# Preparation spread over every second unit, and one running sequence of stages beside a selective-scan loop

## The chip, the cores and the metric

The kernel runs on one core of a Trainium2 chip. The core has a matrix engine (PE), a vector engine (DVE), a scalar engine (ACT), a general engine (POOL) and a queue engine (SP), which here issues almost all DMAs. Each engine works through its own list of instructions in order and waits on semaphores. The metric is device time in microseconds, from start to end of one execution; lower is better. Four timed executions of the kernel before lie between 13899.16 and 13924.62 us, median 13905.3 us.

## The reference

The input is x, float32 of shape (4, 96, 64, 64). Four layers are applied, each as x + layer(group_norm(x)) with 32 groups and no gains:

- layer 0: attention with 3 heads from all 4096 pixels to a 2x2-averaged grid, a 3x3 neighbourhood mix of its result, a 5x5 depthwise term and a projection;
- layer 1: a projection to 2 x 192 channels, a 3x3 depthwise convolution and SiLU, then a selective scan in four directions, a layer norm, a gate, a 1x1 / 3x3 depthwise / 1x1 chain and a squeeze-and-excite factor;
- layer 2: a 3x3 convolution of 96 to 96 channels;
- layer 3: pointwise and depthwise convolutions, a second four-direction scan, a gate, layer norms, a grouped squeeze/expand unit with a softmax over channels, and a projection.

The scans are the bulk. For each image, direction, channel (192) and state (16) a recurrence runs over 4096 positions:

```
h[t] = h[t-1] * exp(delta[t] * A) + delta[t] * u[t] * B[t]
y[t] = sum over 16 states of h[t] * C[t]   (plus a D term)
```

with delta = softplus(dt_w @ x_dbl + dt_b), and x_dbl, B, C from a projection of u. Layer 1 writes the same recurrence as a quotient of cumulative sums.

## The kernel before

There are eight scans, one per image and scan layer, in the order of `SCANS`: layer 1 of images 0 and 1, layer 3 of images 0 and 1, then the same of images 2 and 3. Each has 4 directions x 4 chunks of 1024 positions x 2 halves of the channels = 32 **groups** of 96 channels. A group has 12 **units**; one unit is 8 channels x 16 states = 128 partitions by 1024 positions. So a scan has 384 units and the loop 3072.

`unit(i, ...)` writes out by hand one turn of the loop for all engines:

- SP: `fetch(i + AHEAD)` loads one row block of delta, broadcast to 16 states, into a `rep` tile (L2038, 12 buffers, 512 KB); AHEAD is 4.
- ACT: `decays(i + 2)` makes exp(delta * A) in place (L2046); `carry_on` copies the last column (L2074).
- DVE: `scan(i)` (L2066), then `times_b(i + 1)` (L2059) multiplies the driven term, in PSUM, by B.
- POOL: `times_c(i)` (L2078) multiplies the states by C.
- PE: `drive(i + 2)` spreads delta * u to the partitions (two bf16 matmuls into `bx`); every fourth unit `collect` sums four finished units into `acc`. Once a group `output` moves `acc` to `yo`, and a store (L2114) takes `yo` to DRAM.

Two other streams are generators whose pieces are put between these by `Slots`: a `yield` ends a piece. **Preparation** (`prepare(g)`) makes the next groups' inputs: u is loaded (L1932, `load_u`), projected, and B, C go through DRAM (`rows`, `bc`); then delta is made by ACT (L1982 to L1988) and five POOL operations (L1989, L1991, L1995, L2006, L2009); delta goes to DRAM as `dd`, and delta * u, cut into three bf16 parts (`cut`, `cut2`), goes through `du` to `parts`. Tiles `t_`, `w_`, `delta` have one buffer each. It begins LEAD = 6 units before the end of group g - 2; DMAs are put off by `later(n, f)`, which runs f n units on. **Stages** (`first`, `second`, `third`, `last`) are the convolutional parts of the layers for other images, listed by scan in `BESIDE`. They take the PE time that `PACE[s]` leaves in a unit, in up to three slots per unit: at its head, after `times_b` (ahead of `collect` and `drive`) and after `drive`. A new `Slots` is made at the start of each scan; what is left of its stage is run out 19 units before the scan's end.

A stage's matmuls go to PSUM tiles tagged `one`, of which there are two; `held()` takes one of them for long in attention, `neighbours` and the layer norms. `group_norm_on_scalar` (L1161 on), `layer_norm` (L1261 on) and the gate of `second` (L1687, L1688) have DVE instructions that follow an ACT instruction in the same piece. `directions` (before `second` and `third`) loads the four direction sums of an image by `ungapped`, four DMAs of 24 partitions each (L1121), 64 DMAs in two pieces.

Of the kernel before, what the change touches and what calls it, by code (L numbers as in the profile page):

```python
# [20 lines left out]
R, N = 6, 16  # L21
# [19 lines left out]
PHI_EPS = 1e-12  # L41
PACE = (2.95,3.45,3.45,2.95,2.95,3.45,3.45,3.2)

# [857 lines left out]
def streams(ctx: ExitStack, tc: tile.TileContext, x, wts, cst, out, wat, cat, flag):  # L901
# [139 lines left out]
    def held():  # L1041

        return ps.tile([128, PCH], F32, tag="one", name="held")

# [73 lines left out]
    def ungapped(dst, src, cols):  # L1118

        for q in range(4):  # L1120
            nc.sync.dma_start(out=dst[24 * q : 24 * q + 24], in_=src[32 * q : 32 * q + 24, cols])  # L1121

# [36 lines left out]
    def group_norm_on_scalar(src, dst):  # L1161

        st = small.tile([96, 8], F32, name="gs_st")
        for j in range(4):
            s = src[:, bass.ts(j, CH)]
            nc.scalar.activation(s, s, AF.Copy, accum_out=st[:, j : j + 1])
            yield 1
        mv = small.tile([96, 4], F32, name="gs_mv")
        nc.vector.tensor_reduce(mv[:, 0:1], st[:, 0:4], AX.X, ALU.add)
        yield 0.5  # L1170
        p = bank()
        mm(p[:96, 0:1], group[:96], mv[:, 0:1])
        yield
        nc.scalar.activation(mv[:, 1:2], p[:96, 0:1], AF.Copy, scale=-1.0 / L)
        yield 0.5
        for j in range(8):
            p = bank()
            nc.scalar.activation(p[:96], src[:, bass.ts(j, PCH)], AF.Square, bias=mv[:, 1:2], accum_out=st[:, j : j + 1])
            yield 1
        nc.vector.tensor_reduce(mv[:, 2:3], st, AX.X, ALU.add)  # L1180
        yield 0.5
        p = bank()
        mm(p[:96, 0:1], group[:96], mv[:, 2:3])
        yield
        nc.scalar.activation(mv[:, 2:3], p[:96, 0:1], AF.Sqrt, bias=eps[:96], scale=1.0 / L)
        yield 0.5
        nc.vector.reciprocal(mv[:, 2:3], mv[:, 2:3])
        nc.vector.tensor_mul(mv[:, 3:4], mv[:, 1:2], mv[:, 2:3])
        yield 0.5
        for j in range(4):  # L1190
            nc.scalar.activation(dst[:, 16 * j : 16 * j + 16, :], img(src)[:, 16 * j : 16 * j + 16, :], AF.Identity,
                                 scale=mv[:, 2:3], bias=mv[:, 3:4])
            yield 1
# [67 lines left out]
    def layer_norm(pool, V, n, gains, each, chunks=range(8)):  # L1261
# [30 lines left out]
        nc.scalar.activation(r[:m], acc[:m], AF.Sqrt, bias=eps[:m])  # L1292
        yield n
        nc.vector.reciprocal(r[:m], r[:m])
# [12 lines left out]
    def attention(b, xn, samp, dist):  # L1307

        with Stack(2) as pool:
# [46 lines left out]
            for pair in [((0, e), (1, e)) for e in range(4)] + [((2, 0), (2, 1)), ((2, 2), (2, 3))]:  # L1356
# [24 lines left out]
                for s, (r, e) in enumerate(pair):  # L1381
# [3 lines left out]
                        rs[bass.ts(s, 32)].rearrange("p (a b) -> p a b", b=32),  # L1385
                    )
                yield 1
            yield from pool.clean()

    def neighbours(b, xn, samp, dist, feat):  # L1390


        with Stack(2) as pool:
# [36 lines left out]
            rs = lines[:8]  # L1430
            nc.vector.reciprocal(rs, acc[:8])
            yield 1
            for j in range(8):
# [74 lines left out]
    def directions(pool, b, tag):  # L1508

        V = pool.tile([96, 2, L], F32, name="V", bufs=1)  # L1510
        with Stack(1) as T:
            full = len(groups) // len(SCANS) * (SCANS.index((tag, b)) + 1)
            cols = []
            for h in range(2):
                while stored[0] < full - 1 + h:
                    yield WAIT
                t = T.tile([96, W, H], F32, name="yc", bufs=2)
                cols.append(t)
                for j in range(4):
                    ungapped(t.rearrange("p a b -> p (a b)")[:, bass.ts(j, CH)], y_col[h][b], bass.ts(j, CH))  # L1520
                    ungapped(V[:, h, bass.ts(j, CH)], y_row[h][b], bass.ts(j, CH))
                yield 4

# [18 lines left out]
    def second(b):  # L1542
# [90 lines left out]
        with Stack(1) as R2:  # L1633
# [32 lines left out]
            with Stack(2) as pool:  # L1666
# [3 lines left out]
                for j in range(8):  # L1670
# [15 lines left out]

                    nc.scalar.activation(q[:96], q[:96], AF.Tanh, bias=half_ag2, scale=0.5)  # L1687
                    nc.vector.scalar_tensor_tensor(out=x2, in0=q[:96], scalar=1.0, in1=x2, op0=ALU.add, op1=ALU.mult)  # L1688
                    nc.sync.dma_start(out=skip3[b][:, js], in_=x2)
# [31 lines left out]
    def last(b):  # L1721

        with Stack(1) as PX:
            V = PX.tile([96, 2, L], F32, name="V", bufs=1)
            per_way = 2 * NCH
            first_ = len(groups) - 4 * per_way
            while stored[0] < first_ + 2 * per_way:
                yield WAIT
            with Stack(1) as T:
                for h in range(2):  # L1730
                    t = T.tile([96, W, H], F32, name="yc")
                    for j in range(4):
                        ungapped(t.rearrange("p a b -> p (a b)")[:, bass.ts(j, CH)], y_col[h][b], bass.ts(j, CH))
                    yield 1
                    for j in range(8):
                        nc.scalar.copy(img(V[:, h, bass.ts(j, PCH)]),
                                       t[:, :, 8 * j : 8 * j + 8].rearrange("p a b -> p b a"))
                        yield 1
            yield from finish(PX, b, V, [(first_ + 3 * per_way + 2 * k + 2, (7 - 2 * k, 6 - 2 * k)) for k in range(NCH)])

    def finish(PX, b, V, blocks):

        with Stack(2) as pool:
# [55 lines left out]
            for need, chunks in blocks:  # L1799
                while stored[0] < need:  # L1800
                    yield WAIT
# [134 lines left out]
    def prepare(g):  # L1936

        s, b, tag, k, axis, back, c, h = groups[g]
        if h == 0:
            us = low.pop(g) if g in low else load_u(g)  # L1940
            yield 0

            p = bank()
# [6 lines left out]
            bc = sp.tile([128, 2, CH], F32, name="bc", bufs=2)  # L1950
            at = [slice(64 * e, 64 * e + R + 2 * N) for e in range(2)]
            for e in at:
                nc.scalar.copy(pr[e], p[e])  # L1953

            def to_rows():
                for e in range(2):
                    nc.sync.dma_start(out=rows[:, bass.ts(e, PCH)], in_=pr[at[e]])

# [5 lines left out]

            later(1, to_rows)
            later(3, to_bc)
            yield 2
            low[g + 1] = us, bc
        else:
            us, bc = low.pop(g)  # L1970
            yield 0
            yield 0
# [11 lines left out]
        nc.scalar.activation(w, t, AF.Identity, bias=one[:96])  # L1984
        yield 0
        nc.scalar.activation(delta, w, AF.Identity, bias=minus[:96])
# [3 lines left out]
        yield 0  # L1990
        nc.gpsimd.tensor_tensor(delta, w, t, ALU.add)  # L1991
        yield 0
        dd = dram.tile([96, CH], F32, name="dd", bufs=3)
        later(1, lambda: nc.sync.dma_start(out=dd, in_=delta))
        nc.gpsimd.tensor_tensor(t, delta, time(us[h], back, 0, CH), ALU.mult)  # L1995
        yield 0

        if h == 1 and g + 1 < len(groups) and groups[g + 1][0] == s:
            later(1, lambda: low.update({g + 1: load_u(g + 1)}))


        parts = cuts[g % 2]
# [3 lines left out]
        nc.gpsimd.tensor_tensor(t, t, c0, ALU.subtract)  # L2006
        yield 0
        nc.scalar.copy(c1, t)
        nc.gpsimd.tensor_tensor(c2, t, c1, ALU.subtract)  # L2009
        yield 0  # L2010
        du = dram.tile([96, 3, CH], BF16, name="du", bufs=2)
# [10 lines left out]

        later(1, to_du)
        later(3, to_parts)
        ready[g] = parts, dd, bc
# [89 lines left out]

    AHEAD, BEHIND, LEAD = 4, 2, 6
    DRIVE, SUM, SLOT = 0.43, 1.71, 0.5
    total = len(groups) * NG
    per = total // len(SCANS)
    store, waiting, stored, owed = [], [], [0], 0.0  # L2120

# [11 lines left out]
    def unit(i, prep, work, budget):  # L2133


        if i + AHEAD < total:
            fetch(i + AHEAD)
        while store:
            store.pop()()
            stored[0] += 1  # L2140
        catch_up(1)
        j = i - BEHIND - 3
        due = j >= 0 and j % 4 == 0
        left = budget - DRIVE - (SUM if due else 0.0)
        mine = 1 <= prep.slots <= 3
        left -= prep.begin(1.0) if mine else work.begin(left)
# [10 lines left out]
        work.end()  # L2157
        left -= work.begin(left)
        if due:
# [5 lines left out]
        if due and j % NG == NG - 4:  # L2165
            store.append(output(j))
        work.end()
# [5 lines left out]
    class Slots:  # L2173


        def __init__(self, stage):
            self.stage, self.open, self.slots = stage, False, 0

        def begin(self, left):

            if left < 0.3:
                return 0.0
# [3 lines left out]
            if v == WAIT:  # L2186
                return left
            while isinstance(v, tuple):
# [6 lines left out]
        def end(self):  # L2195
            if self.open:
                self.open = False
                next(self.stage, 0)

# [5 lines left out]

    def beside(s):
        stages = {"first": first, "second": second, "third": third, "last": last}
        for n, b in BESIDE[s]:
            yield from stages[n](b)

    Slots(first(0)).run()
    solo[0] = False
    with tc.manual_schedule():
# [15 lines left out]
        for i in range(total):  # L2229
            s, at = divmod(i, per)  # L2230
            g, m = divmod(i, NG)
            if at == 0:
                work, owed = Slots(beside(s)), 0.0
            if m == NG - LEAD and g + 2 < len(groups):
                prep.run()
                prep = Slots(prepare(g + 2))

            if at == per - NG - LEAD - 1 and s < len(SCANS) - 1:
                work.run()

            owed = min(owed, 0.6) + PACE[s]
            owed = unit(i, prep, work, owed)
        for j in range(total - 4, total, 4):
            collect(j)
            output(j)()
            stored[0] += 1
    solo[0] = True
    spare.clear()
    work.run()

# [48 lines left out]
```

## Time and profile before

| | |
|---|---|
| median of 4 runs | 13905.3 us |
| profiled execution, its own time | 13926.5 us |
| its span | 13924.7 us |
| before the first scan instruction | 661.6 us |
| loop of 3072 units | 661.6 to 13802.6 us |
| after the loop | 122.1 us |
| mean granted TensorE clock | 0.898 |
| DVE / PE / POOL / ACT busy | 84% / 80% / 74% / 62% of the span |
| DMA moved | 2695 MB, mean 194 GB/s |

The eight scans take 1613.3, 1617.9, 1594.4, 1600.3, 1587.9, 1597.1, 1599.6 and 1930.5 us; the last has the stages `third` three times and `last` beside it. How to read it: an engine's busy share is an average over the loop and over 780 us of head and tail in which the scan engine does little. A wait is put to the instruction that ended it; a stretch of time (a window) has the busy time of every engine, and its length less DVE's busy time is DVE's idle time there.

### The profile page before, as it was taken

Reading aid. Unit: us, or ns where it says so; the run is one execution under the profiler, and the core shown is the slowest. Engines: PE = TensorE matmul, PEld = TensorE weight load, DVE = VectorE, ACT = ScalarE, POOL = GpSimd, SP = SyncE. Lnnn points to the kernel's source line nnn. Section 1 sums busy time; section 2 is a strip of 40 time slices with the busy share of each in tenths; the row PEclk is TensorE's granted clock in tenths of the full one; section 3 lists DMA queues with packets and bytes.
Section 4 is the critical chain, followed back from the end, with each engine's and each line's share of the span. In section 5 each row is a group of like instructions: output and inputs, shape, how many; then the busy total and the mean of one; then the engine's idle time right before and its main releaser. Section 6 shows DMA issues by size and latency. Waiting matters only on the chain.

```text
span 13924.7 us, 127815 instructions
## 1 busy us (share of the span) xinstructions
PE 11080.0 (80%) x40137; PEld 3348.7 (24%) x40802; DVE 11634.9 (84%) x7509; ACT 8696.8 (62%) x12314; POOL 10283.0 (74%) x4730
## 2 busy tenths in 40 slices
PE   8878886988779796878868887897969887677756
PEld 3322221322223221222212221232313222111111
DVE  1478988987889888889888899898989989877886
ACT  3366576667756676665766566566856677665654
POOL 1177887877878787788877888787878878666674
PEclk9999998998889897999989998998979998888867
DMA  0267888887878888778877788787888878777774
GB/s 11 64 170 197 203 220 213 205 213 185 226 193 218 214 213 211 187 193 213 222 197 194 194 210 231 189 222 195 224 210 206 221 195 231 185 175 193 184 201 115
DMA packets 846672, 2695.23 MB, mean 194 GB/s; under 512 B 112480, under 2 KB 115008, under 8 KB 845984
## 3 DMA queue, kind: packets, MB, share of 16 engines
q1 hardware_dynamic: 845328, 2685.08, 76.0%
q8 instruction: 324, 5.31, 0.2%
q14 instruction: 364, 2.98, 0.1%
q10 hardware_dynamic: 656, 1.87, 0.0%
HBM read 2186.34 MB, written 500.17 MB: 193 GB/s over the span
## 4 chain that ended last, share of the span: by engine, by line
PE 34%; DVE 24%; ACT 16%; DMA 11%; issue 7%; POOL 7%; SPq 1%; DVEq 0%; POOLq 0%; ACTq 0%; another core or an unknown queue 0%
PE one L1028 20%; DVE hs L2066 15%; PE bx L1028 7%; DVE bx L2059 7%; PE acc L1028 5%; DMA rep<-dd 4%; POOL rep L2078 4%; ACT rep L2046 4%; PE held L1028 2%; ACT L2046 1%; ACT arena L1375 1%; DMA arena<-ycol 1%; DMA du<-cut 1%; DMA parts<-du 1%; ACT L1988 1%
## 5 line engine op out<-in xcount | busy, mean ns | idle before, releaser
L2078 POOL TENSOR_TENSOR rep<-hs,bc 128x1024 f32<-128x1024 f32 x3072 | 7225.6, 2359 | 2587.9 <-DVE hs L2066 2164.7
L1028 PE MATMUL one<-arena 128*96 128x512 f32 (+5 forms) x11072 | 5280.4, 603 | 704.2 <-ACT arena L1375 138.0
L2066 DVE TENSOR_TENSOR_SCAN hs<-rep,carry,bx 128x1024 f32<-128x1024 f32 x2304 | 5400.8, 2344 | 298.2 <-ACT carry L2074 23.7
L2059 DVE TENSOR_TENSOR bx<-bx,bc 128x1024 f32<-128x1024 f32 x3072 | 3717.2, 1210 | 678.2 <-PE bx L1028 494.8
L2046 ACT ACTIVATE rep<-rep,l_decay 128x1024 f32<-128x1024 f32 x3072 | 3496.8, 1143 | 835.0 <-DMA rep<-dd 819.0
L1028 PE MATMUL bx<-parts,spread 128*128 128x512 bf16 x5479 | 1882.6, 419 | 1314.9 <-DVE hs L2066 1191.4
L1028 PEld LDWEIGHTS one<-arena 128*96 128x96 f32 (+4 forms) x11072 | 1795.2, 172 | 3135.5 <-issue 1818.4
L2066 DVE TENSOR_TENSOR_SCAN hs<-rep,bx 128x1024 f32<-128x1024 f32 x768 | 1754.3, 2284 | 136.4 <-ACT carry L2074 56.6
L1028 PE MATMUL acc<-rep,ct 128*32 128x512 f32 x12288 | 1713.8, 671 | 11.3 <-POOL rep L2078 8.1
L1028 PEld LDWEIGHTS <-spread 128*128 128x128 bf16 x6144 | 443.8, 100 | 3631.3 <-DVE hs L2066 2384.1
L1028 PE MATMUL one<-pr,ct 64*96 64x512 f32 x1024 | 627.8, 697 | 92.9 <-ACT pr L1953 38.5
L1375 ACT ACTIVATE arena<-one 128x512 f32<-128x512 f32 x576 | 342.3, 595 | 499.4 <-PE one L1028 497.8
L1028 PEld LDWEIGHTS acc<-rep,ct 128*32 128x32 f32 x12288 | 357.7, 118 | 1161.6 <-issue 932.1
L2046 ACT ACT_TABLE_LOAD x482 | 618.4, 1283 | 8.5
L2074 ACT COPY carry<-hs 128x1 f32<-128x1 f32 x2304 | 408.2, 177 | 228.1 <-DVE hs L2066 226.2
L1028 PE MATMUL bx<-arena 128*96 128x512 f32 (+5 forms) x1120 | 489.1, 576 | 34.9 <-DMA arena<-in_w 16.7
L1028 PE MATMUL one<-arena,ct 128*96 128x512 f32 x508 | 298.2, 696 | 252.1 <-ACT arena L1526 176.5
L1028 PE MATMUL held<-arena,cols 128*32 128x256 f32 x3072 | 482.8, 396 | 12.9 <-ACT arena L1375 11.7
L1028 PE MATMUL held<-arena 128*32 128x256 f32 x3072 | 483.3, 396 | 0.0
L982 POOL MEMSET arena<- 32x1024 f32 (+5 forms) x81 | 54.1, 690 | 403.9 <-ACT arena L1375 331.7
L1028 PE MATMUL one<-us,wt 128*38 128x512 f32 x1024 | 290.3, 689 | 73.6 <-DMA us<-urow 33.7
L1988 ACT ACT_TABLE_LOAD x256 | 328.4, 1283 | 4.4
(3322 smaller groups left out, 9865.0 us busy)
## 6 DMA issues: line engine op xcount, KB each, us to landing
rep<-dd SPq DMA_DIRECT2D x3072, 512.0 KB
parts<-du SPq DMA_DIRECT2D x1024, 144.0 KB
bc<-rows SPq DMA_DIRECT2D x256, 512.0 KB
dd<-delta SPq DMA_DIRECT2D x256, 384.0 KB
du<-cut SPq DMA_DIRECT2D x256, 384.0 KB
yrow<-yo SPq DMA_DIRECT2D x128, 512.0 KB
ycol<-yo SPq DMA_DIRECT2D x128, 512.0 KB
us<-urow SPq DMA_DIRECT2D x128, 384.0 KB
```

What stands on the lines that cost most here:

```text
L982: nc.gpsimd.memset(arena[96:, k : min(k + CH, a + n)], 0.0)
L1028: nc.tensor.matmul(o, lhsT=lhsT, rhs=rhs, start=first, stop=last)
L1375: nc.scalar.activation(last.rearrange("p a b -> p (a b)"), p, AF.Exp, scale=HD**-0.5)
L1988: nc.scalar.activation(w, w, AF.Ln)
L2046: nc.scalar.activation(a, a, AF.Exp, scale=decay[tag][:, k, NG * h + m : NG * h + m + 1])
L2059: nc.vector.tensor_mul(bx, bx, ready[i // NG][2][:, 0, :])
L2066: nc.vector.tensor_tensor_scan(out=hs, data0=a, data1=bx, initial=carry[:, h, m : m + 1] if c else 0.0, op0=ALU.mult, op1=ALU.add)
L2074: nc.scalar.copy(carry[:, h, m : m + 1], live[i][1][:, CH - 1 : CH])
L2078: nc.gpsimd.tensor_tensor(a, hs, ready[i // NG][2][:, 1, :], ALU.mult)
```

## The change

- Preparation: each POOL operation after the second has an empty piece between it and the next; LEAD is 8; `rows` and `bc` are put off by 2 and 4 units. u of the next pair is loaded at the start of the odd group's preparation, also across a scan's end if the stage that writes it is done.
- AHEAD is 5.
- One generator runs all stages in sequence; a stage may begin as soon as the one before is done, and must be done 33 units before the scan's end. PACE is changed. A piece that yields WAIT gives up the rest of that unit.
- WAIT is put between the ACT and the DVE instruction in `group_norm_on_scalar` (once), `layer_norm` (once) and the gate of `second`.
- `directions` and `last` issue their loads one piece a unit, with long rows for the direction that is done first; a load waits until the store of its rows is two units past (`landed`).
- While a `held` tile is in use (`tight`) the middle slot of a unit is skipped.
- The store of `yo` is issued two units after `output`.

```diff
-PACE = (2.95,3.45,3.45,2.95,2.95,3.45,3.45,3.2)
+PACE = (3.03, 3.46, 3.46, 2.76, 2.8, 3.46, 3.46, 3.2)
 def held():
+        tight[0] = True
+    def landed(n):
+        return len(stores) >= n and clock[0] >= stores[n - 1] + 2
 # group_norm_on_scalar, after the four ACT sums
+        yield WAIT
 # layer_norm, after Sqrt of the variances, before the reciprocal
-        yield n
+        tight[0] = False
+        yield WAIT
 # directions
-                while stored[0] < full - 1 + h:
+            while not landed(scanned(tag, b, soon) + 2 * NCH):
+                yield WAIT
+            for h in range(2):
+                for q in range(4):
+                    nc.sync.dma_start(out=flat[soon][h][24 * q : 24 * q + 24],
+                                      in_=image_of[soon][h][b][32 * q : 32 * q + 24, :])
                     yield WAIT
-                for j in range(4):
-                    ungapped(t.rearrange("p a b -> p (a b)")[:, bass.ts(j, CH)], y_col[h][b], bass.ts(j, CH))
-                    ungapped(V[:, h, bass.ts(j, CH)], y_row[h][b], bass.ts(j, CH))
-                yield 4
+            for c in range(NCH):
+                for h in range(2):
+                    while not landed(scanned(tag, b, late) + 2 * c + h + 1):
+                        yield WAIT
+                    js = bass.ts(NCH - 1 - c, CH)
+                    ungapped(flat[late][h][:, js], image_of[late][h][b], js)
+                    yield WAIT
 # second, the gate
                     nc.scalar.activation(q[:96], q[:96], AF.Tanh, bias=half_ag2, scale=0.5)
+                    yield WAIT
                     nc.vector.scalar_tensor_tensor(out=x2, in0=q[:96], scalar=1.0, in1=x2, ...)
 # prepare
-            later(1, to_rows)
-            later(3, to_bc)
+            later(2, to_rows)
+            later(4, to_bc)
         else:
             us, bc = low.pop(g)
-            yield 0
+            if g + 1 < len(groups) and (groups[g + 1][0] == s or done[0] > s):
+                later(1, lambda: low.update({g + 1: load_u(g + 1)}))
             yield 0
...
         nc.gpsimd.tensor_tensor(delta, w, t, ALU.add)
+        dd = dram.tile([96, CH], F32, name="dd", bufs=3)
+        later(2, lambda: nc.sync.dma_start(out=dd, in_=delta))
+        yield 0
         yield 0
         nc.gpsimd.tensor_tensor(t, delta, time(us[h], back, 0, CH), ALU.mult)
         yield 0
-        if h == 1 and g + 1 < len(groups) and groups[g + 1][0] == s:
-            later(1, lambda: low.update({g + 1: load_u(g + 1)}))
+        yield 0
...
         nc.scalar.copy(c0, t)
         nc.gpsimd.tensor_tensor(t, t, c0, ALU.subtract)
         yield 0
+        yield 0
         nc.scalar.copy(c1, t)
         nc.gpsimd.tensor_tensor(c2, t, c1, ALU.subtract)
-        yield 0
...
-        later(1, to_du)
-        later(3, to_parts)
+        later(2, to_du)
+        later(4, to_parts)
-    AHEAD, BEHIND, LEAD = 4, 2, 6
+    AHEAD, BEHIND, LEAD = 5, 2, 8
 # unit
-        while store:
-            store.pop()()
-            stored[0] += 1
         catch_up(1)
-        mine = 1 <= prep.slots <= 3
+        mine = prep.slots <= 2
...
-        left -= work.begin(left)
+        if not tight[0]:
+            left -= work.begin(left)
         if due:
             collect(j)
...
         if due and j % NG == NG - 4:
-            store.append(output(j))
+            later(2, stored(output(j)))
 # Slots.begin
-            if left < 0.3:
+            if left < 0.3 or self.rest == clock[0]:
                 return 0.0
...
             if v == WAIT:
-                return left
+                self.rest = clock[0]
+                return 0.0
 # the loop
-            if at == 0:
-                work, owed = Slots(beside(s)), 0.0
-            if at == per - NG - LEAD - 1 and s < len(SCANS) - 1:
-                work.run()
+            if at == per - 2 * NG - LEAD - 1 and s < len(SCANS) - 1:
+                while done[0] <= s:
+                    work.rest = -1
+                    work.begin(9.0)
+                    work.end()
```

## Prediction

> **What bounds the kernel now.** I read the windows by scan first, then the groups by line. Columns of a window: start:end, length, busy time (and count) of PE, PEld, DVE, ACT, POOL, then PE clock, DMA share, GB/s. The first window is scan 2, the second twelve units (348 to 359) of it in which no stage runs, the third and fourth are discussed below.
>
> ```profile
> 3892.80:5487.20 1594.40, 1324.72 (x4256) 407.49 (x4332) 1406.52 (x876) 1045.06 (x1441) 1268.14 (x571) 0.91 0.84 212
> ...
> 5351.50:5395.80 44.30, 23.84 (x75) 4.05 (x76) 42.78 (x26) 28.08 (x41) 37.89 (x17) 0.65 1.03 252
> ...
> 3900.97:3975.65 74.68, 47.10 (x140) 13.70 (x140) 41.82 (x25) 41.92 (x62) 40.37 (x18) 0.84 0.85 217
> ...
> 5520.60:6165.20 644.60, 533.50 (x2976) 158.43 (x3025) 555.80 (x339) 430.03 (x669) 491.19 (x225) 0.96 0.75 188
> ```
>
> ```profile
> L2066 DVE TENSOR_TENSOR_SCAN hs<-rep,carry,bx 128x1024 f32<-128x1024 f32 x2304 | 5400.8, 2344 | 298.2 <-ACT carry L2074 23.7 <-ACT rep L2046 18.7 <-DVE bx L2059 4.9
> ...
> L2059 DVE TENSOR_TENSOR bx<-bx,bc 128x1024 f32<-128x1024 f32 x3072 | 3717.2, 1210 | 678.2 <-PE bx L1028 494.8 <-PE one L1028 68.7 <-PE acc L1028 63.1
> ```
>
> A unit costs DVE 2.34 + 1.21 us, and where no stage runs a unit takes 44.30 / 12 = 3.69 us with DVE 97% busy: DVE is the floor. Over the eight scans (13141 us) DVE is busy 11415 us and idle 1726 us. The change removes no DVE work, so all it can win is a part of 1726 us, and the question is which idle time it reaches. DVE idles mostly for `bx`, which PE makes late because in its list stage matmuls or `collect` stand ahead of `drive`.
>
> **The change part by part.**
>
> *A, loads of `directions`.* In the timeline of the start of scan 2:
>
> ```profile
> 3907.55 1.16 SPq L2038 DMA_DIRECT2D rep<-dd  x2
> ...
> 3908.89 1.07 ACT L1526 COPY arena<-arena 96x512 f32<-96x512 f32 x1 [10.07 <-DMA arena<-ycol]
> ...
> 3910.01 2.02 PE L1028 MATMUL one<-arena,ct 128*96 128x512 f32 x2 [8.36 <-ACT arena L1526]
> ...
> 3912.92 1.23 DVE L2059 TENSOR_TENSOR bx<-bx,bc 128x1024 f32<-128x1024 f32 x1 [6.09 <-PE bx L1028]
> ...
> 3931.14 0.52 SPq L2038 DMA_DIRECT2D rep<-dd  x1
> ```
>
> SP issues nothing for `rep` for 22 us, and ACT, PE and DVE wait in a row for the first loads. The third window above is these twelve units: 74.68 - 41.82 = 32.9 us idle. The same view gives 32.7, 38.4 and 34.3 us in the three `third` of scan 7; with four `second` that is 4 x 32.9 + 105.4 = 237 us. After, the loads (192 fewer DMAs in all, long rows instead of quarters) go out one piece a unit before the copies begin: counting pieces in both programs, `second` of scan 1 now begins its loads in unit 346 of scan 0, after which no stage ran before. What stays is dense ACT work (41.92 us in twelve units of 43 us): I leave 10 us at each of the seven places and win 167 us (bounds 0 and 237). The cover is spent elsewhere: those units have DMA engines 103% busy and the loads are 6.3 MB, 25 us at 252 GB/s. At seven places that costs 0 to 175 us; a part of the loads finds room in units that also wait for other things, and I take 50.
>
> *B, WAIT ahead of DVE instructions.* From the waits (us, times, longest), with C and E:
>
> ```profile
> DVE arena L1688 <- ACT one L1687: 96.4, 30, 5.8
> ...
> DVE gs_mv L1169 <- ACT arena L1166: 62.7, 9, 13.2
> ...
> DVE lines L1294 <- ACT lines L1292: 22.0, 14, 2.8
> ...
> ACT rep L2046 <- DMA rep<-dd: 819.0, 438, 13.3
> ...
> PEld acc L1028 <- POOL rep L2078: 173.3, 189, 4.4
> ...
> PE bx L1028 <- DMA parts<-du: 97.8, 28, 28.9
> ```
>
> Each of the first three moves to the head of the next unit, some 3.6 us on. The first averages 3.2 us, the third 1.6: I take 92 and 20. The second averages 7.0, so 9 x 3.6 = 32. Sum 144 us (bounds 60 and 181). Behind the waiting instruction stood `scan` and `times_b`, so this is paid on DVE itself. The stage pieces that WAIT pushes on are covered: by the count `second` now ends in unit 346 instead of 337, and must end by 351, so nothing is run out at once.
>
> *C, AHEAD 5.* The 438 waits of ACT average 1.9 us and a unit more of lead is 3.6, so most go. A `rep` load takes, in the chain that ended last (start, length),
>
> ```profile
> 1648.06 10.44 DMA rep<-dd
> ...
> 2610.10 6.97 DMA rep<-dd
> ```
>
> 7 to 10 us where it matters, against the two units (7.2 us) from its `fetch` to its `decays` now, and three after. ACT is 62% busy, so little of it is DVE time: `scan` itself waited 19.5 us for it (8 times); above, the chain's 4.3% of the span, 599 us. Nearest is the direct row, raised for what reaches DVE through PE: 100 us. The twelve buffers stand the lead: a buffer's last reader, `collect`, is two units before the `fetch` in PE's list at the tightest, three before.
>
> The Trainium skill, DMA: Bandwidth & Descriptors, section Anatomy of one DMA, fits a DMA at about 2.0 us plus bytes over 436 GB/s (for another issuing path). By it a 512 KB `rep` is there in an estimated 3.2 us, the old lead is ample, and C would be nil. The two chain pieces above contradict it in this loop, with its engines at 75 to 103%, and the measurement decides.
>
> *D, `tight`.* The fourth window is attention of scan 3 (150 units): 644.60 - 555.80 = 88.8 us idle, near 270 us for three. One of two `one` tiles is held, and a matmul in the middle slot waits for ACT to empty the other with `drive` behind it. Skipping that slot puts `drive` first; in scans 3 and 4 the same work is also spread over 157 and 162 units, in scan 0 pressed into 145. A third, 80 us (bounds 0 and 270).
>
> *E, POOL in every second unit.* POOL has 2.36 us of `times_c` in a 3.60 us unit; an operation of 2.35 more puts it 1.1 us back, five in a row 5.5 us, after at most two in a row, 2.2 us. `collect` waits on POOL 173.3 us on PE. Of this 63.1 (`bx` for `acc`) reach DVE: 40 us. `parts` now lands a unit earlier against its first `drive` (97.8 us on PE): 30 us. Sum 70 (0 and 271).
>
> *F, u ahead.* `us` at a scan's start came late by about a unit, seven times: 20 us (0 and 63, PE's waits for `us` in its group row, 33.7 + 29.7). The two u loads of a pair move ahead of `dd`, `du` and `parts` on SP, which wait for their makers anyway.
>
> *G, what it costs.* The POOL tail of one group now stands two units closer to the next group's first ACT operation on the one `t_` buffer:
>
> ```profile
> 6353.75 2.14 POOL L2009 TENSOR_TENSOR cut<-t__31649,cut 96x1024 bf16<-96x1024 f32 x1
> ...
> 6360.70 0.69 ACT L1982 ACTIVATE t__31881<-one,wt 96x512 f32<-96x512 f32 x1 [0.33 <-PE one L1028]
> ```
>
> It began 4.8 us after POOL was done; 7.2 us less is a wait of 2.4 us. Behind it in ACT's list stand evictions and `decays`; 256 groups x 0 to 3.6 us (a unit) is 0 to 922 us. ACT has idle time, and E makes POOL earlier: 0.3 us a group, 75 us. The store of `yo` moves behind one more `fetch` on SP and a unit nearer to the next load of `yo`, with 2.5 units left, 9 us: nothing, and with that gone about 1 us for 128 loads.
>
> *Sum.* C, D and E meet in the same rows (`bx` for PE: 494.8 + 68.7 + 63.1 = 627 us, which hold part of A too), so I count 185 of their 250. 167 + 144 + 185 + 20 = 516, less 50 and 75, is 391 us. The profiled execution took 13926.5 us, 21 us over the median: 13535 by its own time, 13515 as a median, 2.8% less. Head and tail (780 us) hold the same instructions.
>
> **The rivals.**
>
> *Shallow.* What goes was cover: PE's list is as full as before, so C to E win nothing, and A and B give half. 156 + 20 less 30 for the loads: 13760 us. For it: DVE's direct rows name no DMA. Against: the clog of SP shows itself in one chain from DMA to DVE.
>
> *Deep.* Stalls feed each other (a late `rep` delays an eviction, that `drive`, that the next `collect`), and half of the idle 1726 us goes: 13050 us. For it: the chain that ended last runs only 24% over DVE. Against: units in the quiet middle of scans already take 3.60, so the gain must come from few places.
>
> *Slower.* G decides: ACT loses time in each of 256 groups, and the `decays` behind it come late. It pays back all the gain of 466 us at 1.8 us a group; at a full unit it is 922 - 466 = 456 us slower, 14360 us. For it: the gap of 4.8 us above is shorter than the two units taken. Against: after C the `rep` tiles are there earlier and `decays` runs two units ahead of its scan.
>
> *It doesn't do what it says.* WAITs starve the stages and a rest is run out in one go before the scan's end. The count of pieces rules it out in scans 0 to 6; in scan 7 the stages wait for the scan as before. What is left is a gain that G just cancels: near 13905.
>
> **How the numbers follow.** A measurement of this kernel tells 0.2% (28 us) from no change. Likeliest, 13380 to 13660: 0.50. Shallow, 13660 to 13877: 0.24. Deep, under 13380: 0.13. No change: 0.04. Slower: 0.09. The range 13200 to 13800 leaves out about 0.05 below, and above it slower, no change and the last of shallow. Faster 0.87, same 0.04, slower 0.09.
>
> **What would show it.** A: no gap without `rep` loads at scan starts, and those twelve units near 50 us. B: the first wait under 10 us. C: ACT's wait for `rep` under 250 us. D: attention's idle under 0.5 us a unit. E: the PE waits on POOL and `parts` under half. G: a wait of ACT for `cut` on POOL at the line that L1982 becomes, over 500 us if the slower case holds. Wrong if DMA latency grows with the shorter loop so that the longer lead is eaten, or if the idle time moves to another wait on PE.

## The result and the profile after

The changed kernel takes 13913.5 us (median of 32 runs) against 13905.4 us before: a ratio of 1.0006, 95% interval 1.0001 to 1.0011. That is 8 us more where 391 us less was forecast; by the bound of 0.2% it is no change. The profiled execution of after has a span of 13941.0 us, 16 us more than that of before. The loop alone is 22 us longer: head and tail are 660.3 and 117.7 us, a little less than before, and DVE is busy 11628.2 us against 11634.9 before. So this is a question of where idle time went.

The eight scans of after take 1650.4, 1604.4, 1652.4, 1550.3, 1538.5, 1596.5, 1654.4 and 1913.8 us. Stages have moved across the scans' ends, so they are not compared one by one; the windows are. These are after's windows (start:end, length, busy time and count of PE, PEld, DVE, ACT, POOL, then clock, DMA share, GB/s): scan 2; units 346 to 383 of scan 1, where `second` of scan 2 now issues its first loads and waits; the copies of `directions` (ten units); `layer_norm` behind them (22 units); the attention of scans 2 and 3 (157 units).

```profile
3915.10:5567.45 1652.35, 1381.75 (x4679) 439.00 (x4762) 1426.27 (x900) 1096.71 (x1538) 1276.71 (x581) 0.93 0.80 203
3742.94:3915.10 172.16, 75.83 (x239) 13.26 (x242) 135.39 (x80) 80.62 (x97) 124.49 (x55) 0.62 0.93 234
3941.04:3990.29 49.25, 37.02 (x110) 11.17 (x111) 34.86 (x20) 40.78 (x56) 31.32 (x14) 1.00 0.69 169
3990.29:4116.98 126.69, 91.53 (x267) 22.49 (x271) 109.28 (x93) 62.99 (x94) 77.26 (x34) 0.92 0.62 154
5415.40:6083.52 668.12, 542.80 (x3022) 159.63 (x3070) 574.55 (x352) 439.73 (x657) 512.68 (x224) 0.95 0.75 187
```

The same units 346 to 383 before, when no stage ran in them:

```profile
3745.51:3892.77 147.26, 76.81 (x253) 13.48 (x250) 135.68 (x80) 78.51 (x97) 121.79 (x54) 0.64 0.90 223
```

Length less DVE's busy time is its idle time. The copies of `directions` have 49.25 - 34.86 = 14.4 us of it, where the twelve units before had 32.9: the gap at the start of the scan is gone, as forecast. But at the scan's end the idle time went from 11.6 to 36.8 us. What was won is paid 40 units earlier. Attention has 93.6 us in 157 units, 0.60 a unit, as before.

The waits that answer to those shown of before (engine, tile, line, then what ended the wait; us, times, longest), and the two groups of DVE:

```profile
ACT rep L2067 <- DMA rep<-dd: 757.2, 275, 11.1
PE bx L1028 <- DMA parts<-du: 192.2, 24, 28.5
DVE hs L2087 <- ACT carry L2095: 118.2, 63, 9.7
PEld acc L1028 <- POOL rep L2099: 75.7, 87, 2.7
DVE arena L1714 <- ACT one L1712: 70.6, 20, 6.7
DVE gs_mv L1183 <- ACT arena L1179: 52.7, 10, 17.0
```

```profile
L2087 DVE TENSOR_TENSOR_SCAN hs<-rep,carry,bx 128x1024 f32<-128x1024 f32 x2304 | 5401.7, 2344 | 413.6 <-ACT carry L2095 103.8
L2080 DVE TENSOR_TENSOR bx<-bx,bc 128x1024 f32<-128x1024 f32 x3072 | 3716.3, 1210 | 573.0 <-PE bx L1028 366.8
```

DVE waits 105 us less ahead of `times_b` (573.0 against 678.2) and 115 us more ahead of `scan` (413.6 against 298.2); of this rise 80 us are put down to `carry` (103.8 against 23.7). The timeline of after at the end of scan 0 (units 350 to 353) shows how:

```profile
2150.65 0.52 SPq L2059 DMA_DIRECT2D rep<-dd  x1
...
2151.64 0.29 SPq L1537 DMA_DIRECT2D arena<-yrow  x1
...
2155.44 0.52 SPq L2059 DMA_DIRECT2D rep<-dd  x1
...
2157.62 0.29 SPq L1537 DMA_DIRECT2D arena<-yrow  x1
2157.68 1.15 ACT L2067 ACTIVATE rep<-rep,l_decay 128x1024 f32<-128x1024 f32 x1 [7.70 <-DMA rep<-dd]
...
2165.23 1.15 ACT L2067 ACTIVATE rep<-rep,l_decay 128x1024 f32<-128x1024 f32 x1 [6.32 <-DMA rep<-dd]
...
2166.55 2.35 DVE L2087 TENSOR_TENSOR_SCAN hs<-rep,carry,bx 128x1024 f32<-128x1024 f32 x1 [4.08 <-ACT carry L2095]
```

A load of `directions` now stands between every two `rep` loads. Counting the instructions of each kind from the start, the `decays` at 2157.68 is that of unit 352, whose `rep` was issued at 2146.14, 11.5 us before; for unit 353 it is 16.4 us, for units 354 to 358 it is 19 to 22. A `decays` stands two units ahead of its `scan` (7.7 us in unit 346); in units 352 to 359 it begins 1.32 us before it, with only its own 1.15 us and the copy of a carry behind it in ACT's list (hence the releaser's name). The lead is used up, and DVE waits for a DMA.

### The profile page after: what moved, and what is told of

Read it like the earlier page. It is cut to its first block, busy times and chain, and to the rows that moved or that the text cites. A ratio compares the mean times of both kernels' runs of the same rounds, so it can differ in the third digit from the quotient of the medians.

```text
span 13941.0 us, 127304 instructions
## 1 busy us (share of the span) xinstructions
PE 10941.5 (78%) x40143; PEld 3316.0 (24%) x40802; DVE 11628.2 (83%) x7509; ACT 8720.2 (63%) x12305; POOL 10283.1 (74%) x4730
## 4 chain that ended last, share of the span: by engine, by line
PE 39%; DVE 25%; ACT 14%; DMA 11%; issue 5%; POOL 3%; SPq 1%; DVEq 0%; POOLq 0%; ACTq 0%; another core or an unknown queue 0%
PE one L1028 24%; DVE hs L2087 17%; PE bx L1028 8%; DVE bx L2080 7%; PE acc L1028 6%; DMA rep<-dd 3%; ACT rep L2067 3%; DMA parts<-du 2%; PE held L1028 2%; POOL rep L2099 2%; ACT L2067 1%; DMA arena<-yrow 1%; ACT arena L1390 1%; ACT L2012 1%; ACT delta L2010 1%
## 5 line engine op out<-in xcount | busy, mean ns | idle before, releaser
L2087 DVE TENSOR_TENSOR_SCAN hs<-rep,carry,bx 128x1024 f32<-128x1024 f32 x2304 | 5401.7, 2344 | 413.6 <-ACT carry L2095 103.8
L2080 DVE TENSOR_TENSOR bx<-bx,bc 128x1024 f32<-128x1024 f32 x3072 | 3716.3, 1210 | 573.0 <-PE bx L1028 366.8
L2067 ACT ACTIVATE rep<-rep,l_decay 128x1024 f32<-128x1024 f32 x3072 | 3496.8, 1143 | 767.0 <-DMA rep<-dd 757.2
L2087 DVE TENSOR_TENSOR_SCAN hs<-rep,bx 128x1024 f32<-128x1024 f32 x768 | 1754.1, 2284 | 98.8 <-ACT carry L2095 14.4
L1028 PE MATMUL acc<-rep,ct 128*32 128x512 f32 x12288 | 1675.5, 662 | 5.0 <-POOL rep L2099 4.1
L1028 PE MATMUL one<-pr,ct 64*96 64x512 f32 x1024 | 593.9, 662 | 100.1 <-ACT pr L1977 43.2
L1395 DVE RECIPROCAL arena<-held 64x256 f32<-64x256 f32 x24 | 42.0, 1749 | 317.0 <-PE held L1028 317.0
```

The lines of the kernel that those rows point to most:

```text
L1028: nc.tensor.matmul(o, lhsT=lhsT, rhs=rhs, start=first, stop=last)
L1395: nc.vector.reciprocal(rs, av[:64, :Q])
L2067: nc.scalar.activation(a, a, AF.Exp, scale=decay[tag][:, k, NG * h + m : NG * h + m + 1])
L2080: nc.vector.tensor_mul(bx, bx, ready[i // NG][2][:, 0, :])
L2087: nc.vector.tensor_tensor_scan(out=hs, data0=a, data1=bx, initial=carry[:, h, m : m + 1] if c else 0.0, op0=ALU.mult, op1=ALU.add)
```

## The experiments

Every ratio is to the kernel before, run beside it. Differences between two experiments are those of their medians and good to some 15 to 25 us. There are two series: parts of the change added to the kernel before, and parts taken from the kernel after. Not tried alone were PACE, the later store of `yo` and the load of u across a scan's end; they stand in the step "one sequence of stages". The idle time of DVE by stage below counts each unit (from one `scan` instruction to the next) to the stage whose piece the program placed in it, from one profiled execution each, in us; rows can trade some 25 us, by how the units at a stage's edge are counted:

| units with | before | before + B, C, E to G | after | after, no slot skipped | all three mends |
|---|---|---|---|---|---|
| copies of `directions` | 237 | 244 | 124 | 132 | 131 |
| no stage, or `second` and `third` loading and waiting | 107 | 51 | 220 | 191 | 122 |
| `layer_norm` and `finish` | 232 | 231 | 281 | 232 | 226 |
| attention | 271 | 276 | 269 | 247 | 244 |
| body of `second` (taps, gate) | 405 | 384 | 440 | 434 | 448 |
| `group_norm` | 119 | 136 | 114 | 109 | 111 |
| the rest | 356 | 312 | 305 | 295 | 277 |
| sum | 1727 | 1634 | 1753 | 1640 | 1559 |

### Parts taken from after

**Stages held to their own scan** (`own_scan`):

```diff
         for s in range(len(SCANS)):
+            while clock[0] < s * per:
+                yield WAIT
             for n, b in BESIDE[s]:
```

> The kernel after, with every stage held back until its own scan begins (as before the change): no load of a later scan runs at the end of a scan. Ends theory: the change won at the starts of scans (idle of the directions stages 237 us before, 124 us after) and paid the same at their ends, where the loads meet DMA engines already 95 to 103% busy (idle of units that wait for or issue these loads 202 us after, against 106 us in the stage-free units before). Then the ends return to some 3.9 us a unit, 5 x 35 us = 175 us less, and the starts take the loads back, 110 to 180 us more: 13860 to 13930 us, no clear gain. Rival, the loads are cheap and something else eats the gain: the starts cost 167 us more and the ends give back under 50 us, so 14020 us or more. Second rival, it was bad to let stages cross the scans at all: 13780 us or less.

Measured 14153.1 us, ratio 1.0175 (1.0161 to 1.0189). It looks like the first rival, but its profile tells another story: the stages don't end by unit 351 of their scan any more, and what is left is run out at once. Units 348 to 359 of scan 3 in this kernel:

```profile
6973.73:7092.79 119.06, 95.09 (x252) 31.92 (x253) 42.90 (x26) 49.78 (x66) 44.92 (x20) 0.90 0.44 119
```

That is 9.9 us a unit; a unit without a stage takes 3.7. Over the same twelve units of six scans the excess over 3.7 us is some 210 us (9.9 and 9.2 us a unit in scans 3 and 4, 5.1 to 5.2 in the four `second`). After has an excess there too: units 348 to 371 of these six scans take 742 us here and 733 in after. So the ends give nothing back, and the 240 us that this kernel takes more than after stand mostly at the starts: units 0 to 71 of scans 1 to 7 take some 200 us more. The run doesn't decide between the theories, as the run-out hides what the ends would give back; what it shows is that loads issued one a unit need the time before the scan.

**The old preparation** (`prep_back`): `prepare`, LEAD 6 and `mine` as before, all else as after.

```diff
-    AHEAD, BEHIND, LEAD = 5, 2, 8
+    AHEAD, BEHIND, LEAD = 5, 2, 6
-        mine = prep.slots <= 2
+        mine = 1 <= prep.slots <= 3
```

> The kernel after, with the old preparation (its GpSimd operations in consecutive units, u loaded as before, lead of 6 units, old distances of its loads and stores). Theory that the preparation costs what the rest wins (term G, and parts, for which PE's wait rose from 98 to 192 us): 13780 to 13860 us. My terms E and F (90 us less 75 us for G) say 13930 us. Rival, the new preparation is the part that works: 13990 us or more.

Measured 13911.4 us, ratio 1.0002 (0.9993 to 1.0011): nothing either way, so the preparation is not what eats the gain. PE's wait for POOL goes back to 180.9 us, and ACT's wait for `rep` falls from 757.2 to 483.2 us without any gain in time.

**No WAITs** (`no_waits`): the three `yield WAIT` ahead of DVE instructions taken out.

> The kernel after, without the three new WAITs (group_norm, layer_norm, gate). My term B says 144 us more: 14060 us. Rival, the wait only changes its place (DVE's idle in the gate's units fell by 5 of 60 us a scan and rose by 6 us a scan in layer_norm): 13890 to 13950 us.

Measured 13981.2 us, ratio 1.0051 (1.0037 to 1.0064): 68 us more than after, half of term B, more than the rival.

**Fetch four ahead** (`ahead4`): `AHEAD` 4 again.

> The kernel after, with fetch four units ahead as before. My term C says 100 us more: 14015 us. Rival, the lead is eaten because the DMA engines and the in-order issuing of SP set when a rep lands, not the unit in which it is asked for (ACT's wait for rep only fell from 819 to 757 us): 13890 to 13945 us.

Measured 13987.1 us, ratio 1.0059 (1.0045 to 1.0072): 74 us more than after. ACT's wait for `rep` is 1208.9 us there, against 757.2 in after.

So B and C are worth 142 us in after, the preparation nothing, and after is still no faster than before: something in it costs. The next runs looked for that.

**No slot skipped** (`no_tight`):

```diff
     def held():
-        tight[0] = True
```

> The kernel after, with the middle slot never skipped (tight is never set). My term D says 80 us more: 13995 us. Rival, tight costs, because the skipped slots press the same work into the others (attention's idle was 271 us before and 269 after): 13840 us. Second rival, nothing: 13890 to 13940 us.

Measured 13841.9 us, ratio 0.9956 (0.9943 to 0.9970): `tight` costs 72 us where term D counted a gain of 80. Its windows for the scan's end and for `layer_norm` of scan 2, which answer to the second and fourth of after:

```profile
3703.05:3865.35 162.30, 73.58 (x244) 13.06 (x242) 135.30 (x80) 80.58 (x97) 124.43 (x55) 0.64 0.95 245
3940.59:4057.24 116.65, 90.69 (x272) 21.99 (x271) 108.53 (x94) 63.08 (x94) 77.74 (x34) 0.92 0.67 167
```

The same 22 units of `layer_norm` have 8.1 us of idle time instead of 17.4. `layer_norm` holds a `one` tile too, and there the skip makes its subtraction on DVE wait for the matmul before it (first after, then this run, one line further up):

```profile
DVE arena L1294 <- PE one L1028: 92.9, 63, 6.8
...
DVE arena L1293 <- PE one L1028: 48.3, 29, 6.5
```

The same wait is 53.0 us before, and in every kernel that skips no slot in `layer_norm` between 43 and 55 us; with the skip it is 86 to 127 us. The rise of 45 us is most of the 72.

**Slots skipped in attention and `neighbours` alone** (`tight_att`, on top of the 4 KB packets described next):

```diff
-    def held():
+    def held(near=True):
-        tight[0] = True
+        tight[0] = near
 # layer_norm
-        acc = held()
+        acc = held(False)
```

> The kernel after with 4 KB packets, slots skipped in attention but not in layer_norm. By the idle time in layer_norm of second (73 us with slots skipped, 33 us without) the skip costs 40 of its 72 us there and the rest in attention and in units that wait: 13825 us. Theory that attention, for which I had counted a gain, gains nothing and loses nothing and all the cost is in layer_norm: 13792 us. Theory that attention is what costs: 13864 us, as with 4 KB packets alone.

Measured 13819.6 us, ratio 0.9930 (0.9916 to 0.9943). The same kernel with all skips takes 13864.4, with none 13792.5: of the 72 us, 45 are `layer_norm`'s (the wait of its subtraction is 43.5 us here). The other 27 (13 by the ratios) are at the edge of what these runs tell; a gain in attention near the 80 us that I had counted is excluded. In attention's units the profiles of after and `no_tight` show both sides: with the skip DVE waits some 24 us less ahead of `times_b`, as term D meant, and some 48 us more for the held tile, ahead of the sums into `yo` and ahead of `scan`.

### The loads at the scans' ends

**4 KB packets** (`short_rows`): the same bytes in the same units, cut by columns; `last` likewise.

```diff
                 for q in range(4):
-                    nc.sync.dma_start(out=flat[soon][h][24 * q : 24 * q + 24],
-                                      in_=image_of[soon][h][b][32 * q : 32 * q + 24, :])
+                    js = bass.ts(q, CH)
+                    ungapped(flat[soon][h][:, js], image_of[soon][h][b], js)
                     yield WAIT
```

> The kernel after, with the pieces of the directions loads cut by columns instead of by rows: the same 384 KB a unit in the same units, but as 4 loads of 24 packets of 4 KB where after sends one load of 24 packets of 16 KB. Packet theory: in the trace of after a 16 KB packet takes 1.21 us (median) and 13.3 GB/s an engine, a 4 KB packet 0.25 us and 16.2 GB/s, and 24 long packets lie unevenly on 16 engines, so that the rep packets behind them are late; the units 348 to 371 of seven scan ends took 5.2 us instead of 3.7. Then most of that goes: 100 to 250 us less than after, 13665 to 13815 us. Rival, the DMA engines are full there and only the bytes count: 13890 to 13940 us. Second rival, SP's issuing is the limit (24 more issues a stage): 13950 us or more.

Measured 13864.4 us, ratio 0.9969 (0.9957 to 0.9981): 50 us less than after, half of the low end expected, but below both rivals. The profile's DMA records agree: after has 1536 more packets of 16 KB than before (8 x 8 x 24 rows), and these run at 13.2 GB/s an engine against 16.2 of the 4 KB packets (in units 348 to 371 of scan 1 alone 13.0 against 15.7). Units 348 to 371 of scan 1 went from 120.2 to 110.3 us (92.9 before), so a dearer part was left. Of the seven ends that the expectation counted, only five hold loads: at the ends of scans 2 and 3 after runs an early `first` in these units.

The Trainium skill, DMA: Bandwidth & Descriptors, section Rules for kernel authors, advises to coalesce many small transfers into a large one. These runs differ, at sizes above the 64 KB under which that row of the page speaks of mostly overhead: 32 loads of 96 KB beat 8 of 384 KB by 50 us. The loads and their packets became shorter together, so which of the two counts is not shown.

**The first eight pieces every third unit** (`spread_rows`, with 4 KB packets) and **the same with 16 KB packets** (`spread_long`):

```diff
                     ungapped(flat[soon][h][:, js], image_of[soon][h][b], js)
-                    yield WAIT
+                    for _ in range(3):
+                        yield WAIT
```

> The kernel after with 4 KB packets, its first eight directions pieces begun every third unit instead of every unit (the same bytes over 24 units of the scan's end, where DMA engines are full without them). Theory that the bytes are what is left of the price: the same as with a piece a unit, 13850 to 13880 us. Rival, the burst is what is left (384 KB a unit beside the 512 KB of rep): most of the 14 us a scan end goes, 13790 to 13830 us.

> The kernel after with its 16 KB packets kept, but the first directions pieces begun every third unit. If the size of the packets is a cost by itself: 39 us less than after, 13875 us. If long packets only hurt because they come in every unit: as with 4 KB packets and the same spread, 13825 us.

Measured 13825.4 us (0.9946, 0.9932 to 0.9959) and 13880.5 us (0.9982, 0.9972 to 0.9991). With 4 KB packets the spread wins another 39 us, so the bytes were not what was left. With long packets it wins 33 us, to the 13875 of the packet theory. Size (of packet and load) and density are separate costs: 50 to 55 us for the size, 33 to 39 for the density. Units 348 to 371 of scan 1 take 95.5 and 97.0 us. The size then shows little there, and most of the 48 us between the two profiled spans lies in scans 5 to 7 (9, 18 and 17 us).

### Parts added to before

**Fetch five ahead alone** (`b_ahead5`): `AHEAD` 5 in the kernel before.

> The kernel before with fetch five units ahead and nothing else. My term C: ACT's wait for rep goes from 819 to under 250 us and the time falls by 100 us, 13805 us. Rival, that wait goes as said but is not what DVE waits for: 13885 to 13910 us, and DVE's wait for bx from PE rises instead.

Measured 13867.2 us, ratio 0.9974 (0.9965 to 0.9983): 36 us less, a third of term C. Its waits:

```profile
DVE bx L2059 <- PE bx L1028: 515.1, 251, 17.0
ACT carry L2074 <- DVE hs L2066: 393.6, 222, 6.2
ACT rep L2046 <- DMA rep<-dd: 269.3, 122, 12.4
...
DVE hs L2066 <- ACT carry L2074: 24.6, 10, 11.5
```

ACT's wait for `rep` fell by 550 us, as forecast. 167 us of it came back as ACT's wait for the scan's result (226.2 before): ACT was early. DVE's wait ahead of `scan` for `carry` fell by 56 us, its wait for `bx` rose by 20: together 36, as much as the medians differ (the two profiled executions differ by 45).

**The WAITs alone** (`b_waits`, with the rest to the next unit of `Slots`):

```diff
+        yield WAIT
         mv = small.tile([96, 4], F32, name="gs_mv")
...
-        yield n
+        yield WAIT
         nc.vector.reciprocal(r[:m], r[:m])
...
+                    yield WAIT
                     nc.vector.scalar_tensor_tensor(out=x2, in0=q[:96], ...)
```

> The kernel before with the three WAITs and nothing else. My term B: 144 us less, 13760 us, the first wait from 96 to under 10 us. Rival, the instruction that waited stands a unit later behind the same dense ACT, and most of its wait stays (in before with the WAITs and the longer lead it was still 77 us): 13865 to 13890 us.

Measured 13912.8 us, ratio 1.0003 (0.9994 to 1.0012): nothing.

```profile
DVE bx L2061 <- PE one L1028: 95.5, 65, 6.1
DVE arena L1690 <- ACT one L1688: 73.7, 23, 6.7
...
DVE gs_mv L1170 <- ACT arena L1166: 44.1, 8, 9.2
...
DVE lines L1295 <- ACT lines L1293: 21.4, 13, 2.8
```

The three waits fell from 181 to 139 us, not to 37: a unit later ACT is still not done with the instruction before, as the rival said. And `times_b` waits 27 us more for PE's `one`.

**WAITs and five ahead** (`b_wa`):

> The kernel before, with two parts of the change alone: the three WAITs (with the rest to the next unit that they need) and fetch five units ahead. If these two are worth there what taking them from after cost (68 and 72 us): 13765 us. My terms B and C: 13660 us. Rival, they only mend what the rest of the change spoils: 13890 to 13930 us.

Measured 13862.4 us, ratio 0.9971 (0.9962 to 0.9980): 41 us, the sum of the two alone (36 and nothing), and not the 142 that they are worth in after.

**With the new preparation** (`b_wap`): `b_wa` with `prepare`, LEAD 8 and `mine` of after.

> The kernel before with the WAITs, fetch five ahead and the new preparation, and nothing else (no slot skipped). If the preparation is worth nothing either way, as in after: 13850 to 13875 us, and the 64 us that the kernel with the old sequence took more are the skipped slots. Rival, those 64 us are the preparation: 13925 us. My terms E, F and G: 13847 us.

Measured 13823.4 us, ratio 0.9933 (0.9920 to 0.9947): 39 us less than `b_wa`, better than both theories and my terms. In the table this is mostly the idle time of units without a stage, 51 us against 107 before (96 in `b_wa`). Its waits for POOL and for `parts` are half of before's 173.3 and 97.8 or less:

```profile
PEld acc L1028 <- POOL rep L2075: 87.9, 97, 5.6
...
PE bx L1028 <- DMA parts<-du: 38.9, 5, 28.5
```

ACT's wait for `rep` doubled at the same time, from 226.5 us in `b_wa` to 505.9, and yet the kernel is faster.

**And with skipped slots** (`old_seq`): `b_wap` with `tight`, so everything but the one sequence of stages.

> The kernel before, with everything of the change but the one sequence of stages: preparation, WAITs, tight and fetch five ahead are in; loads in bursts at the scan's start, stores and PACE are the old ones. Theory that the sequence with its loads is what costs: 13765 us or less (13905 less 68 and 72). Rival, tight or the rest costs and the sequence gains its 117 us of term A: 14030 us.

Measured 13926.2 us, ratio 1.0014 (1.0005 to 1.0023): 103 us more than `b_wap`. In idle time `layer_norm` and `finish` go from 231 to 303 us (the wait of the subtraction from 45.1 to 115.3), attention stays at 276 and 277.

### The mends together

`short_notight` is after with 4 KB packets and no skipped slot; `spread_notight` also has the first pieces every third unit.

> The kernel after with both mends found so far: pieces of the directions loads with 4 KB packets (50 us less than after) and no slot skipped (72 us less). If they are independent: 13792 us. Rival, both free the same idle time at the scan ends and in the layer_norm units: 13825 us or more.

> The kernel after with three mends: 4 KB packets, the first directions pieces begun every third unit, no slot skipped. If independent: 13792 less 39, 13753 us. Rival, the spread and the unskipped slots free the same idle time: 13780 us or more.

Measured 13792.5 us (0.9921, 0.9907 to 0.9935) and 13756.6 us (0.9890, 0.9875 to 0.9905). The mends add up, and the last kernel is 149 us faster than before. Its window for units 346 to 383 of scan 1, with nearly the same bytes as in after (39.0 MB against 40.2):

```profile
3701.93:3853.87 151.94, 73.87 (x239) 12.94 (x242) 135.61 (x79) 78.71 (x95) 128.74 (x56) 0.64 0.96 257
```

Idle time is 16.3 us, against 36.8 in after and 11.6 before the change, and the bytes come at 257 GB/s instead of 234.

The way from before to after, each step a run: 13905, fetch five ahead 13867, WAITs 13862, preparation 13823, one sequence of stages with its loads 13842, skipped slots 13914. Up to `b_wap` the change wins 0.67%; the skipped slots (+72 us, +70 by the ratios) give most of it back, and the sequence (+19, +32, at the edge of what these runs tell) the rest.

## Why the prediction was wrong

**The step that failed most is D**, "A third, 80 us (bounds 0 and 270)". The sign is wrong: the skip costs 72 us in after and 103 on the old sequence. I costed the skip by what it puts first (`drive`) and for attention only, and its lower bound excluded a loss without a reason. What lost the skipped slot was not followed: the pieces have to stand in two slots instead of three, and `layer_norm` also holds a tile. There DVE's subtraction now waits for its matmul, 92.9 us against 48.3, a rise of 45 of the 72 us. Attention has 0.58 us of idle time a unit in after (269 in 464 units); under 0.5 was claimed.

**A: most of the gain came, the price was too low.** 113 us of idle time went from the copies (167 forecast). For the price I wrote "0 to 175 us; a part of the loads finds room in units that also wait for other things, and I take 50". Measured against `b_wap`, the kernel with the old loads, these units went from 51 to 191 us without skipped slots, 140 us, within the bounds. Two parts of the price were not in the count of bytes, the long packets and a load in every unit. With both mended the units have 122 us, some 70 more than `b_wap`, near the 50 taken, and the sequence gains 67 us over `b_wap` (13756.6 against 13823.4), against 117 for A. The "seven places" were not alike either: the four `second` and the first `third` load in the last units of a scan, the other two `third` inside scan 7, whose DMA share before was 0.73 and not 1.03.

**B, 144 us:** 0 alone, 68 undone in after. The step "Each of the first three moves to the head of the next unit, some 3.6 us on", took ACT to be done within that unit, but most of the wait is still there a unit later; the first wait was claimed to fall under 10 us and is 70.6.

**C, 100 us:** 36 alone, 74 undone in after. The wait went as claimed (269 us alone, 250 forecast), but its worth was "raised for what reaches DVE through PE", and PE gave nothing: DVE's wait for `bx` rose. In after the wait is 757 us, not under 250. That is near what I had named as "DMA latency grows [...] so that the longer lead is eaten", only that it isn't the shorter loop that did it. Two parts of the change did: the loads of A (some 400 of the 757 us stand in units in which they are issued or waited for) and the new preparation (226.5 to 505.9 us on the old sequence, and 757.2 to 483.2 where it is taken from after). C was costed on a loop without either. But ACT's wait is a poor measure of the time: the kernel with the three mends still has 789.9 us of it and is 157 us faster than after. What fell there is DVE's wait for `carry`, from 118.2 to 35.3 us.

**E, F and G:** 70 + 20 less 75 was forecast; 39 (53 by the ratios) was measured on the old sequence and nothing in after. E was right in its place: PE's wait for POOL fell by half, that for `parts` by more; with the one sequence of stages the latter is 192.2 us, and 195.4 with the old preparation too. G, the term that carried the slower rival, is nil. At the line that L1982 became, this is what ACT waited for in after (us, times):

```profile
  PE one L1028: 547.3, 320
  POOL cut L2031: 5.6, 3
```

The step "7.2 us less is a wait of 2.4 us" was read off one group and took ACT as ready at that moment; ACT waits there for PE's projection, which comes later than POOL.

**The sum** held gains that the profile of before could show as waits, and for the places where nothing stood in it yet, prices near the low end of their bounds. No rival ended near 13914 us for the right reason: the one at 13905 had stages starved, or G cancelling the gain, and neither was so.

Left open: why the WAITs and the lead are worth 142 us in after and 41 in before (in after the three waits themselves fall by only some 32 us for the 68 that the WAITs are worth), why the preparation wins 39 us in `b_wap` and nothing in after, and why the body of `second` has 50 us more idle time with the one sequence (434 against 384).

## What to carry to other kernels

Cost what a change displaces as carefully as what it puts first: a skipped slot is work that stands elsewhere, and a load moved off a busy spot lands on another stream's deadline. Where a window already shows DMA engines at 90 to 100%, expect bytes put there to cost time, and try short packets and wide spacing: here these two took the idle time of the units that load and wait from 191 to 122 us. A wait taken off an engine is worth only what its follower was late by: follow it along that engine's list to the bound before counting it.

## What the hardware showed

- A packet of 16 KB, one row to one partition, took 1.21 us in the median (95% under 1.81), 13.2 GB/s an engine; 4 KB packets took 0.25 us, 16.2 GB/s. Long packets in large loads cost 50 to 55 us here at equal bytes.
- A busy share near 1 doesn't say what DMA engines deliver: the same 38 units, with nearly equal bytes and no slot skipped, have 245 GB/s at a share of 0.95 with long packets in each unit and 257 GB/s at 0.96 with short ones spread; in the worst 54 us of after (2146 to 2200) it is 210 at 0.95.
- In those 54 us the granted clock was 0.56, with PE busy 21.9 us of them; in the copies of `directions` it was 1.00, with PE busy 37.0 of 49.3 us. In these windows the clock is low where PE has little to do, not where it is pressed.
